# Layer 0's attention order worked out by a planner from a table; initial loads and boundary loads put in another order

## The chip, the cores and the metric

The kernel runs on one core of one Trainium2 chip. Its engines are TensorE (PE), VectorE (DVE), ScalarE (ACT), GpSimd (POOL) and SyncE (SP, which here only issues DMAs). The metric is the device time of one execution in microseconds.

## The reference, cut to what matters

Sixteen samples of 128 channels by 32x32 pixels (1024 tokens) pass through two blocks, each a mixing step and a second step, both with residuals:

```
x = x + linear_attention(group_norm(layer_norm_c(x)))      # layer 0
t = t + stu(layer_norm(t))          # t: x as 1024 tokens
x = x + conv3x3_block(layer_norm_c(x))                     # layer 1
t = t + routed_experts(layer_norm(t))
```

The attention of layer 0 makes queries, keys and values by a 128x128 projection, takes a softmax of the queries over tokens and of the keys within each of four heads, forms a 32x32 context for each head, applies it to the queries and projects the result. The STU is a causal convolution of the tokens with 16 spectral filters, through a Fourier transform, followed by learned 128x128 matrices, plus three taps of direct matrices:

```
U = irfft(rfft(phi) * rfft(u));  out = sum_k U_k s_k M_phi[k]     # plus and minus filters
out = out + sum_i shift(u, i) @ M_u[i]
```

The STU is computed for the first 1024, 512, 256 and 128 tokens with four sets of matrices and mixed with weights. Layer 1 applies two 3x3 convolutions with batch norm and ReLU, then an expert layer: a softmax over tokens for each of 64 experts, the eight largest tokens of each, and two matrices for each expert.

## The kernel before, in words

**Layer 0, attention stage** (0 to 395.7 us). One sample is an object of the class `Attention`, whose methods are its operations, each a handful of instructions on one engine. In order of dependence: `tokens` (eight transposes on PE of 128x128), `moments`, `tokens_copy`, `variance`, `root`, `scales`, `norm` (the layer norm, one ACT instruction for each block of 128 columns, L141), `spread`, `group`, `group_var`, `group_root`, `group_scale` (the group norm's scale), `channels` (transposes back), `channels_copy` (which yields `xn`, L409), `q_`, `q_max`, `q_exp`, `k`, `k_max`, `k_sub`, `k_exp`, `k_sum`, `k_recip`, `k_scale` (on POOL, L461), `q_tokens`, `q_copy`, `context` (PE, L482), `context_mask`, `fold`, `fold_copy`, `fold2`, `fold2_copy` (which fold the values' and the output's weights into one 128x128 matrix), `out`, `out_add`. Then the STU's forward part: `input` (transposes), `input_copy` (ACT, L530), `moments2` to `norm2`, `even` and `odd` (PE, the Fourier transform of the even and odd residue classes of time, L551), copies and sums on ACT and DVE, `even_turns` to `odd_turns4` (butterflies on POOL, which end with the store of the spectrum to `vd` in DRAM, L607), `taps_in` (transposes, L159 as a helper's line), `taps_copy`, `taps` (24 matmul records a sample, L618) and `taps_add` (DVE, L625, then the store of x to `xd`, L626).

The order of the work is written out by hand: `period` (L713) has 62 entries, each an operation and a depth, and the loop at L731 runs periods, doing in period p each operation for sample p + depth. PE, DVE, ACT and POOL execute in the program's order (`manual_schedule(engines=PINNED)`); SP isn't pinned there, and a scheduler of the framework places its DMAs. PSUM is three tiles of 128x1024 (`big`) and two small ones (`s`).

Two generators are stepped by the same loop. `filters()` (L628), once a period at the entry `filters`, negates half the filter's table (`wfm`), transforms the filters (even and odd matmuls at L636), and then loads and scales one of 16 parts of the spectral matrices in each step: the load of `mi` (L662) is issued in the step before the one that uses it (L665, L667). `prepare()` (L671), one step at the start of each period, loads the convolution weights (`raw`), scales and combines them on POOL (L683 to L693), stores them in DRAM as `cwd`, and scales the table of the inverse transform (`pwi`, L703, stored as `wid`).

At the start SP issues the loads of x0, x1, `wf`, `phi`; later x loads are issued by `tokens`, two samples ahead, into eight buffers.

**Layer 0, generation and multiplication** (395.7 to 684.3 us, L746 to L842): in 16 chunks c of frequencies, PE generates the filter's matrices and multiplies the samples' spectra by them; each chunk's products are stored to `yd` by two DMAs of 512 KB (L839). The last two chunks' products go into `yd[1]`.

**Boundary** (684.3 to 723.9 us): SP loads `wi` (the inverse transform's table, from `wid`), `cw` (convolution weights, from `cwd`) and small vectors. `load(b)` (L940) loads a sample's x from `xd` and its products y in two parts: part 0 from the first fourteen chunks (L945, 896 KB), part 1 from the last two (128 KB). For sample 0 the x and part 0 go through POOL's queue, the rest through SP's.

**Layer 1**: the class `Routed` has the operations of one sample, and `table` (L1263) lists each of them with engine, estimated duration, due time, what it depends on, which buffers it opens and closes. `planned` (L1475) plays a list schedule: of the operations that could start within 0.25 us of the earliest, it takes the one due first (due plus b times the period, 54.66), and returns all of them in the order of their planned starts. `ready` gives the earliest time for operations without dependencies. The loop at L1345 then issues them, SP pinned too. The first operations of a sample are `even` (POOL, L958), `odd`, `odd_turn`, `odd_out` (DVE, L965 to L985), `inverse` (PE, L1039), `add` (DVE, L1048) and `tokens`; the convolutions are L926. The experts (L1367 to L1472) follow.

Of the kernel before, what the change touches and what calls it, by code (L numbers as in the profile page):

```python
# [1 line left out]

# [6 lines left out]
F32 = mybir.dt.float32  # L9
# [57 lines left out]
def metaformer_kernel(ctx: ExitStack, tc: tile.TileContext, io: dict, out: bass.AP):  # L67
# [96 lines left out]
    with ExitStack() as l0:  # L164
# [41 lines left out]


        with ExitStack() as a0:
# [96 lines left out]
            for b in range(2):  # L305
                load(b)
            wqk = aconst.tile([P, 2 * C], F32, name="wqk")
# [16 lines left out]
            nc.vector.tensor_scalar(mu[:, 0], mu[:, 0], wmix[:, 0:1], None, ALU.mult)  # L324
            for i in range(1, NF):
                nc.vector.scalar_tensor_tensor(
                    mu[:, i], mu[:, i], wmix[:, i : i + 1], mu[:, i - 1], ALU.mult, ALU.add
                )

# [11 lines left out]
            class Attention:  # L341
# [10 lines left out]
                def tokens(self):  # L352
                    if self.b + 2 < B:
                        load(self.b + 2)
                    self.x = xt[self.b]
                    self.pt = big().rearrange("p (j c) -> p j c", c=C)
                    transpose_in(self.pt, self.x)
# [34 lines left out]
                def norm(self):  # L392
                    normalize(self.tok, self.tok, self.sts[:, 0], self.sts[:, 3])
# [19 lines left out]
                def q_(self):  # L413
# [17 lines left out]
                def k(self):  # L431
# [69 lines left out]
                def fold2(self):  # L501

                    self.pw = ps.tile([P, P], F32, name="pw", tag="s")
                    nc.tensor.matmul(self.pw, wv, self.wy, start=True, stop=True)

                def fold2_copy(self):
# [39 lines left out]
                def norm2(self):  # L546
                    normalize(self.ub, self.ub, self.sts2[:, 0], self.sts2[:, 3])
# [64 lines left out]
                def taps(self):  # L612

                    self.pa = big()
                    for si, (lo, hi) in enumerate(SEGS):
                        for tap in range(KU):
                            a = max(lo, tap)
                            nc.tensor.matmul(  # L618
                                self.pa[:, a:hi], mu[:, NF - 1 - si, tap, :],
                                self.u[:, a - tap : hi - tap],  # L620
                                start=(tap == 0), stop=(tap == KU - 1),
                            )
# [5 lines left out]
            def filters():  # L628

                wfm = setup.tile([P, NQ // 2, 2 * P], F32, name="wfm", tag="mi")  # L630
                nc.vector.tensor_scalar(wfm, wf[:, 1::2, :], -1.0, None, ALU.mult)

                def values(q, dst):
                    for sgn in range(2):
                        w = wfm[:, q // 2, :] if sgn and q % 2 else wf[:, q, :]
# [4 lines left out]
                yield  # L640
                xf = spectrum_tile()
                for parity in range(2):
                    pe = class_values(parity, values)
                    t = class_copy(pe, 1)
                    ts = class_copy(pe, ROT) if parity else t
                    ab = class_sums(parity, pe, t)
                    class_differences(parity, ab, pe, ts)
                    yield
                    for part in range(2):
                        butterflies(ab, xf, parity, part)  # L650
                    if parity:
                        butterflies(ab, xf, 1, butterflies(ab, xf, 1, 2))
                    yield
                half = CW // 2
                e, o = (xf[:, :, i].rearrange("p c r m j -> p c (r m j)") for i in range(2))
                nc.vector.tensor_tensor(ph[:, :, :half], e, o, ALU.add)
                nc.vector.tensor_tensor(ph[:, :, half:], e, o, ALU.subtract)
                for m in range(EPR // MB):
                    es = slice(m * MB, (m + 1) * MB)
                    for i in range(NF):  # L660
                        mi = setup.tile([P, MB, C], F32, name="mi", tag="mi")
                        nc.sync.dma_start(mi, io["M_phi"][i, :, es, :])  # L662
                        yield
                        if i == 0:
                            nc.vector.tensor_scalar(mst[:, es, :], mi, coef[:, 0:1], None, ALU.mult)  # L665
                        else:
                            nc.vector.scalar_tensor_tensor(  # L667
                                mst[:, es, :], mi, coef[:, i : i + 1], mst[:, es, :], ALU.mult, ALU.add
                            )

            def prepare():  # L671
# [36 lines left out]
            nc.sync.dma_start(wf, io["wf"])  # L708
            phi = spool.tile([P, NQ, 2, P], F32, name="phi", tag="xf")
            nc.sync.dma_start(phi, io["phi"])  # L710


            period = (  # L713
                ("q_max", 3), ("out_add", 1), ("tokens", 6), ("moments", 6), ("context", 2),
                ("channels", 4), ("input", 1), ("norm2", 0), ("context_mask", 2),
                ("group_root", 4), ("k_exp", 3), ("fold", 2), ("group_scale", 4), ("moments2", 1),
# [884 lines left out]
```

## Time and profile before

Three runs took 1327.79, 1319.41 and 1328.11 us; the median is 1327.79.

| | us |
|---|---|
| profiled execution, its own time | 1324.0 |
| its span | 1322.2 |
| PE busy | 1216.7 (92%) |
| DVE busy | 907.2 (69%) |
| ACT busy | 705.2 (53%) |
| POOL busy | 503.3 (38%) |
| attention stage, 0 to 396: PE busy | 359.6 of 396 |
| generation and multiplication, 396 to 684: PE busy | 278.5 of 288 |
| boundary, 684 to 724: PE busy | 19.5 of 40 |
| layer 1's convolutions and routing, 724 to 1212: PE busy | 475.1 of 488 |
| experts and output, 1212 to 1322: PE busy | 84.1 of 110 |

Rows of the timeline read: start, duration, engine, line of the kernel, instruction, output <- input, size, count; in brackets how long the engine was idle before and what released it. Matmuls overlap, so differences of starts, not the durations, give PE's work. Where the line of a helper stands (L132 statistics, L141 normalization, L149, L154 and L159 transposes, L232 and L241 sums), the tile's name tells the operation. A chain row has start, length and what it was.

### The profile page before, as it was taken

The page shows a single profiled execution, that of the slowest core. Times are in us where ns is not written, and L with a number is a line of the kernel's source. Part 1 is how long each engine was busy: PE and PEld are TensorE (multiplying, and loading weights), DVE is VectorE, ACT ScalarE, POOL GpSimd, SP SyncE. Part 2 cuts the span into 40 slices and gives each one's busy share as a digit, 9 for nine tenths or more (in the row PEclk, how much of TensorE's full clock was granted, in tenths as well). Part 3 has the DMA queues.
Part 4 walks back from the last instruction along what each step waited for, and adds up shares of the span by engine and source line. Part 5 has one row for each costly group of instructions (what it writes and reads, how often), then busy time and mean ns, then how long its engine had stood idle before and what let it go on. Part 6 is the DMA issues. An engine that isn't in the chain of part 4 may idle for free. (4 is left out here: it accounts for less than half of the span.)

```text
span 1322.2 us, 33734 instructions
## 1 busy us (share of the span) xinstructions
PE 1216.7 (92%) x14116; PEld 990.8 (75%) x14116; DVE 907.2 (69%) x1982; ACT 705.2 (53%) x1424; POOL 503.3 (38%) x816
## 2 busy tenths in 40 slices
PE   4889999999998999999956999999999999996886
PEld 3777777777767888888846987989888888883443
DVE  5688887877765666776637767777778676772224
ACT  3777777777545666666623435545555454544111
POOL 2324545454685777777743111222212121110002
PEclk8899999999998999999987999999999999997998
DMA  7014343433344333333367211313122113007986
GB/s 268 17 35 140 118 134 112 144 124 121 114 149 145 127 125 127 127 121 119 107 235 182 70 48 49 88 27 111 32 80 64 33 49 127 17 24 260 374 329 255
DMA packets 87401, 162.99 MB, mean 123 GB/s; under 512 B 5584, under 2 KB 40784, under 8 KB 86864
## 3 DMA queue, kind: packets, MB, share of 16 engines
q1 hardware_dynamic: 86608, 158.33, 36.2%
q8 instruction: 111, 1.82, 0.6%
q0 software_dynamic: 640, 2.49, 0.5%
q14 instruction: 42, 0.34, 0.1%
HBM read 104.18 MB, written 56.62 MB: 122 GB/s over the span
## 5 line engine op out<-in xcount | busy, mean ns | idle before, releaser
L926 PE MATMUL pcv<-v,cw 128*128 128x256 f32 x1536 | 342.9, 380 | 0.0
L926 PEld LDWEIGHTS pcv<-v,cw 128*128 128x128 f32 x1536 | 286.8, 190 | 42.2 <-issue 5.7
L785 ACT COPY g<-pg 128x512 f32<-128x512 f32 x288 | 153.1, 591 | 102.8 <-PE pg L776 102.8
L783 DVE COPY g<-pg 128x512 f32<-128x512 f32 x224 | 145.8, 687 | 90.1 <-PE pg L776 90.1
L776 PE MATMUL pg<-ph,mst 32*128 32x128 f32 x4096 | 155.3, 287 | 4.5 <-ACT g L785 3.0
L776 PEld LDWEIGHTS pg<-ph,mst 32*128 32x128 f32 x4096 | 130.7, 190 | 30.8 <-issue 25.9
L796 PE MATMUL py<-g,v 128*32 128x128 f32 x4096 | 140.1, 276 | 3.8 <-POOL v L768 1.2
L796 PEld LDWEIGHTS py<-g,v 128*32 128x32 f32 x4096 | 105.3, 110 | 20.7 <-issue 2.4
L767 POOL TENSOR_TENSOR v<-xc 128x256 f32<-128x256 f32 x128 | 91.6, 741 | 71.6 <-PE py L796 62.5
L141 ACT ACTIVATE tok<-tok,sts 128x128 f32<-128x128 f32 x256 | 101.8, 481 | 23.8 <-POOL sts L1001 20.4
L132 DVE BATCH_NORM_STATS2 bst<-big 128x6 f32<-128x256 f32 x256 | 91.1, 417 | 19.5 <-PE big L154 12.1
L1066 POOL TENSOR_SCALAR sts<-bst 128x8 f32<-128x8 f32 x16 | 6.5, 406 | 235.7 <-DVE bst L132 235.7
L920 DVE TENSOR_TENSOR v<-pads 128x544 f32<-128x544 f32 x128 | 85.0, 723 | 9.9 <-ACT pads L1119 9.5
L618 PE MATMUL big<-u,mu 128*128 128x128 f32 (+4 forms) x384 | 86.0, 380 | 0.0
L274 POOL TENSOR_TENSOR xf<-ab 128x256 f32<-128x256 f32 x34 | 24.8, 730 | 132.0 <-DVE ab L241 131.9
L618 PEld LDWEIGHTS big<-u,mu 128*128 128x128 f32 x384 | 56.7, 191 | 18.0 <-issue 15.4
L1097 ACT ACTIVATE ct<-pcv,bn 128x256 f32<-128x256 f32 x64 | 30.3, 474 | 68.8 <-PE pcv L926 67.9
L551 PE MATMUL big<-wf,ub 128*128 128x256 f32 x256 | 62.0, 385 | 0.2
L149 PEld LDWEIGHTS big<-ident,x 128*128 128x128 f32 x384 | 47.3, 148 | 19.2 <-issue 7.2
L149 PE MATMUL big<-ident,x 128*128 128x128 f32 x384 | 53.6, 286 | 8.5 <-DVE x L1048 3.4
L1115 DVE TENSOR_TENSOR r<-pcv,cs 128x256 f32<-128x256 f32 x64 | 26.9, 420 | 49.0 <-PE pcv L926 48.2
L141 ACT ACTIVATE tt<-tt,sts 128x128 f32<-128x128 f32 x128 | 51.1, 480 | 9.2 <-POOL sts L1001 8.9
(231 smaller groups left out, 2271.3 us busy)
## 6 DMA issues: line engine op xcount, KB each, us to landing
we<-in_weight SPq DMA_DIRECT2D x32, 1024.0 KB, 9.7
vd<-xf SPq DMA_DIRECT2D x16, 1024.0 KB, 5.1
xc<-vd SPq DMA_DIRECT2D x64, 256.0 KB, 3.5
yd<-ys SPq DMA_DIRECT2D x32, 512.0 KB, 3.8
y<-yd SPq DMA_DIRECT2D x15, 896.0 KB, 6.5
x<-in_x SPq DMA_DIRECT2D x16, 512.0 KB, 4.1
mi<-in_M_phi SPq DMA_DIRECT2D x16, 512.0 KB, 4.9
xd<-x SPq DMA_DIRECT2D x16, 512.0 KB, 6.0
```

The lines of the kernel that those rows point to most:

```text
L132: nc.vector.bn_stats(bst[:, j : j + 2, :].rearrange("p j s -> p (j s)"), src[:, j : j + 2, :].rearrange("p j c -> p c j"),)
L141: nc.scalar.activation(dst[:, j, :], src[:, j, :], AF.Identity, bias=nm[:, j : j + 1], scale=r[:, j : j + 1],)
L149: nc.tensor.transpose(pt[:, j, :], src[:, j * P : (j + 1) * P], ident)
L551: nc.tensor.matmul(dst, self.ub[:, q, :], wf[:, q, :], start=True, stop=True)
L618: nc.tensor.matmul(self.pa[:, a:hi], mu[:, NF - 1 - si, tap, :], self.u[:, a - tap : hi - tap], start=(tap == 0), stop=(tap == KU - 1),)
L767: nc.gpsimd.tensor_tensor(vv[:, x, 1:, bs], e, o, op)
L776: nc.tensor.matmul(pg[r][:, i], mst[rs, 4 * q + i, :], ph[rs, c, :], start=True, stop=True,)
L783: nc.vector.tensor_copy(dst, src)
L785: nc.scalar.copy(dst, src)
L796: nc.tensor.matmul(py[rows, x, kl, :], v[:, (x * NM + m) * JL + jl, 1 - ri : 3 - ri, :] .rearrange("p k b -> p (k b)"), g[:, ((x * 2 + ri) ...
L920: nc.vector.tensor_tensor(v[:, k], d[i], d[j], op)
L926: nc.tensor.matmul(pc[:, i], wt[:, dy, k, :], v[:, k, hf * HR + dy : hf * HR + dy + HR], start=(dy == 0), stop=(dy == 2),)
```

## The change

1. The attention's order comes from a second `table` and `planned`; `period`, the depths and `filters()` are gone. `norm`, `norm2` and `taps` are cut into two operations each; the filters' steps become operations `f_mixes` to `f_values` (once) and `f_matrix` (sixteen times, load and use in one operation), and `prepare` an operation that takes two steps of its generator. `ready` gives arrival times to the operations that need loads. `q_`, `k` and `fold2` are renamed `queries`, `keys` and `refold`. The filters' steps use the same PSUM and work buffers as the samples.
2. SP's loads at the start are issued as x0, x1, `wf`, `phi`, x2 to x7; from sample 8 on, `tokens` issues the load of the sample two ahead, as before.
3. At the boundary x0 and part 0 of y0 go through SP's queue, ahead of the store of the second-last chunk; `wi` follows, and `cw` comes after y1. SP's resulting order is: small vectors, x0, y0 part 0, store of chunk 14, `wi`, store of chunk 15, y0 part 1, x1, y1, `cw`, x2, y2. Before it was: `gw` and others, `wi`, `cw`, store of chunk 14, store of chunk 15, y0 part 1, x1, y1, x2, y2.
4. Layer 1's `table` has other due times, its period is 51.23, and `ready` is 7 + 5 min(b, 3) for every sample.
5. `planned` passes the operation's name to `ready` and frees a tile only if it was opened; `perform` replaces the list of two-part names; `Routed.x` and `.y` become properties.

The order that `planned` gives for the attention begins as follows on three engines (operation.sample; prepare.k is the k-th pair of steps):

```
PE:   tokens.0 tokens.1 group.0 channels.0 f_even.0 group.1 queries.0 keys.0 tokens.2 q_tokens.0 channels.1 f_odd.0 group.2 queries.1 keys.1 tokens.3 context.0 q_tokens.1 fold.0 channels.2 tokens.4 queries.2 refold.0 q_tokens.2 context.1 out.0 fold.1 group.3 keys.2 input.0
DVE:  ... k_sum.0 k_recip.0 variance.2 scales.2 spread.2 f_matrix.0 f_matrix.1 group_var.2 f_odd_sums.0 q_max.1 group_scale.2 k_max.1 q_recip.1 context_mask.0 k_sub.1 f_values.0 k_sum.1 q_max.2 k_recip.1 fold_copy.0
POOL: f_even_turns.0 prepare.0 prepare.1 k_scale.0 prepare.2 prepare.3 prepare.4 f_odd_turns.0 prepare.5 prepare.6 prepare.7 prepare.8 k_scale.1 prepare.9 prepare.10 prepare.11
```

and a later period on PE is: `out.7 group.10 channels.9 tokens.11 input.7 queries.9 context.8 keys.9 fold.8 q_tokens.9 taps0.6 taps_in.7 refold.8 taps1.6 even.7 odd.7`.

The diff, cut to its core:

```diff
             for b in range(2):
                 load(b)
+            nc.sync.dma_start(wf, io["wf"])
+            phi = spool.tile([P, NQ, 2, P], F32, name="phi", tag="xf")
+            nc.sync.dma_start(phi, io["phi"])
+            for b in range(2, 8):
+                load(b)
...
                 def tokens(self):
-                    if self.b + 2 < B:
+                    if 8 <= self.b + 2 < B:
                         load(self.b + 2)
...
-                def norm(self):
-                    normalize(self.tok, self.tok, self.sts[:, 0], self.sts[:, 3])
+                def norm(self, i):
+                    half = NT // 2
+                    normalize(
+                        self.tok, self.tok, self.sts[:, 0], self.sts[:, 3], i * half, (i + 1) * half
+                    )
 
...
+                def taps(self, i):
+
+                    if i == 0:
+                        self.pa = big()
+                    taps(self.pa, mu, self.u, i)
 
...
+                def f_odd_sums(self):
+                    fl.ao = class_sums(1, fl.po, fl.ot)
+                    class_differences(1, fl.ao, fl.po, fl.os)
+
+                def f_odd_turns(self):
+                    for part in range(2):
+                        butterflies(fl.ao, fl.xf, 1, part)
+                    butterflies(fl.ao, fl.xf, 1, butterflies(fl.ao, fl.xf, 1, 2))
+
+                def f_values(self):
+                    half = CW // 2
+                    e, o = (fl.xf[:, :, i].rearrange("p c r m j -> p c (r m j)") for i in range(2))
+                    nc.vector.tensor_tensor(ph[:, :, :half], e, o, ALU.add)
+                    nc.vector.tensor_tensor(ph[:, :, half:], e, o, ALU.subtract)
+
+                def f_matrix(self):
+                    m, i = divmod(self.b, NF)
                     es = slice(m * MB, (m + 1) * MB)
-                    for i in range(NF):
-                        mi = setup.tile([P, MB, C], F32, name="mi", tag="mi")
-                        nc.sync.dma_start(mi, io["M_phi"][i, :, es, :])
-                        yield
-                        if i == 0:
-                            nc.vector.tensor_scalar(mst[:, es, :], mi, coef[:, 0:1], None, ALU.mult)
-                        else:
-                            nc.vector.scalar_tensor_tensor(
-                                mst[:, es, :], mi, coef[:, i : i + 1], mst[:, es, :], ALU.mult, ALU.add
-                            )
+                    mi = setup.tile([P, MB, C], F32, name="mi", tag="mi")
+                    nc.sync.dma_start(mi, io["M_phi"][i, :, es, :])
+                    if i == 0:
+                        nc.vector.tensor_scalar(mst[:, es, :], mi, coef[:, 0:1], None, ALU.mult)
+                    else:
+                        nc.vector.scalar_tensor_tensor(
+                            mst[:, es, :], mi, coef[:, i : i + 1], mst[:, es, :], ALU.mult, ALU.add
+                        )
+
+                def prepare(self):
+                    for _ in range(2):
+                        next(preparing, None)
+
+            fl = SimpleNamespace()
 
...
-            period = (
-                ("q_max", 3), ("out_add", 1), ("tokens", 6), ("moments", 6), ("context", 2),
...
+            def ready(b, name):
+
+                if name == "tokens":
+                    return 2.0 * b if b < 2 else 8.5 + 1.5 * b
+                if name == "f_matrix":
+                    return 25.0 + 6.0 * b
+                if name == "prepare":
+                    return 22.0 + 3.0 * b
+                return inputs.get(name, 0.0)
+
+            inputs = dict(f_mixes=6.5, f_negate=6.0, f_even=9.5, f_odd=9.5)
+
+            table = (
+                ("tokens", "PE", 0.88, -286.5, "", "big:X x", ""),
...
+                ("k_scale", "POOL", 1.95, -245.9, "k_recip", "", ""),
+                ("context", "PE", 1.77, 119.9, "q_copy k_scale", "s:c", "ke qt"),
+                ("context_mask", "DVE", 0.32, -62.7, "context q_recip", "", "s:c"),
...
+                ("input_copy", "ACT", 1.02, -368.2, "input moments2", "ub", "big:u"),
...
+                ("taps_in", "PE", 0.88, -435.1, "norm21", "big:U", "ub"),
+                ("taps_copy", "ACT", 1.02, -453, "taps_in", "u", "big:U"),
...
+                ("taps 0", "PE", 2.65, 233.5, "taps_copy f_mixes", "big:r", "u"),
+                ("taps 1", "PE", 2.65, -270.1, "taps0", "", "u"),
+                ("taps_add", "DVE", 1.25, -336.2, "taps1", "", "big:r x"),
...
+                ("f_odd_turns", "POOL", 5, -143, "f_odd_sums f_even_turns", "sd:f", "ab1:f sd:f"),
+                ("f_values", "DVE", 4.5, -272.1, "f_odd_turns", "", "xf:f"),
+                ("f_matrix", "DVE", 1.4, 82.7, "", "", ""),
+                ("prepare", "POOL", 1.7, -52, "", "", ""),
             )
-            reach = max(d for _, d in period)
-            samples, setting, preparing = {}, filters(), prepare()
+            buffers = dict(mi=2, big=3, x=8, tok=3, xn=3, qe=2, ke=2, qt=2, ub=2, u=2, et=2, ets=1, ab0=2, ab1=2, sd=2, xf=2, s=2)
+
...
             with tc.manual_schedule(engines=PINNED):
-                for p in range(-reach, B):
-                    next(preparing, None)
-                    for name, d in period:
-                        b = p + d
-                        if name == "filters":
-                            next(setting, None)
-                        elif 0 <= b < B:
-                            if name == "tokens":
-                                samples[b] = Attention(b)
-                            getattr(samples[b], "q_" if name == "q" else name)()
+                for b, name in planned(
+                    table, buffers, B, 102.38, left_out, ready
+                ):
+                    if b not in samples:
+                        samples[b] = Attention(b)
+                    perform(samples[b], name)
...
         wi = first.tile([P, NQ, 2, P], F32, name="wi", tag="wi")
-        nc.sync.dma_start(wi, wid)
         cws = first.tile([P, 2, 3, 4, C], F32, name="cw", tag="cw")
         cw = [cws[:, n] for n in range(2)]
-        for n in range(2):
-            nc.sync.dma_start(cw[n], cwd[n])
...
+        def load_x(b):
+            if b not in loaded:
+                loaded.add(b)
+                xt[b] = xpool[b > 0].tile([P, N], F32, name=f"x{b}", tag=f"x{b}")
+                nc.sync.dma_start(xt[b], xd[b])
+
+        def load_y(b, i):
+            js = (slice(P - 2 * JL), slice(P - 2 * JL, P))[i]
+            if i == 0:
+                yts[b] = first.tile([P, 2, 2 * NM, C], F32, name="y", tag="y", bufs=2)
+            nc.sync.dma_start(
+                yts[b][js].rearrange("p r x e -> p r (x e)"),
+                yd[i][:, :, b].rearrange("j r x e -> j r (x e)"),
+            )
+
         def load(b):
-            xt[b] = xpool[b > 0].tile([P, N], F32, name=f"x{b}", tag=f"x{b}")
-            (nc.sync if b else nc.gpsimd).dma_start(xt[b], xd[b])
-            yts[b] = first.tile([P, 2, 2 * NM, C], F32, name="y", tag="y", bufs=2)
-            for i, js in enumerate((slice(P - 2 * JL), slice(P - 2 * JL, P))):
-                (nc.gpsimd if b + i == 0 else nc.sync).dma_start(
-                    yts[b][js].rearrange("p r x e -> p r (x e)"),
-                    yd[i][:, :, b].rearrange("j r x e -> j r (x e)"),
-                )
-
+            load_x(b)
+            for i in range(2):
+                load_y(b, i)
+
+
+        loaded = set()
+        load_x(0)
+        load_y(0, 0)
+        nc.sync.dma_start(wi, wid)
 
 
...
+        def ready(b, name):
+            return 7.0 + 5.0 * min(b, 3)
+
+        order = planned(table, buffers, B, 51.23, left_out, ready)
         with tc.manual_schedule(engines=PINNED | {mybir.EngineType.SP}):
-            for b in range(2):
-                load(b)
+            load_y(0, 1)
+            load(1)
+            for n in range(2):
+                nc.sync.dma_start(cw[n], cwd[n])
             samples = [None] * B
             for b, name in order:
...
-            if closers[o] == 0:
+            if closers[o] == 0 and o in held:
                 slot, i = held.pop(o)
```

## The prediction

> **What bounds the kernel now.** I first read busy time by stage (columns: stretch and length, then busy us and instructions of PE, PEld, DVE, ACT, POOL, then clock, DMA share, GB/s).
>
> ```profile
> 0.00:66.00 66.00, 44.28 (x207) 35.87 (x208) 38.72 (x138) 36.58 (x78) 19.39 (x32) 0.87 0.38 143
> 66.00:102.00 36.00, 31.68 (x203) 25.36 (x202) 30.49 (x82) 26.67 (x55) 11.55 (x16) 1.00 0.10 32
> 102.00:318.00 216.00, 209.21 (x1247) 164.14 (x1246) 175.35 (x423) 155.87 (x323) 103.96 (x166) 1.00 0.41 128
> 318.00:396.00 78.00, 74.42 (x407) 56.74 (x409) 54.48 (x98) 42.59 (x86) 51.18 (x87) 1.00 0.43 135
> ```
>
> In the attention stage PE is the bound from 102 us on; DVE, next, has 19% spare. Only the fill (0 to 102) is loose. The timeline of DVE gives the period: the first, second, tenth and eleventh samples' `taps_add`.
>
> ```profile
> 100.26 1.23 DVE L625 TENSOR_TENSOR x<-big,x 128x1024 f32<-128x1024 f32 x1 [1.28 <-PE big L618]
> 122.14 1.23 DVE L625 TENSOR_TENSOR x<-big,x 128x1024 f32<-128x1024 f32 x1 [1.28 <-PE big L618]
> ...
> 297.24 1.23 DVE L625 TENSOR_TENSOR x<-big,x 128x1024 f32<-128x1024 f32 x1 [1.27 <-PE big L618]
> 318.25 1.22 DVE L625 TENSOR_TENSOR x<-big,x 128x1024 f32<-128x1024 f32 x1 [1.35 <-PE big L618]
> ```
>
> So (297.24 - 100.26) / 9 = 21.89 us per sample. From start to start in PE's timeline one sample's work is 20.77 us (taps 5.21, the four projections and the context 1.7 to 1.8 each, even and odd 1.75, five transposes 0.88, the rest 0.6). About 1.1 us of each period is idle. The largest piece shows in the waits of PE from 102 to 318:
>
> ```profile
> PE big L159 <- ACT ub L530: 6.6, 10, 0.7
> ```
>
> `taps_in` waits 0.7 us in each of ten periods, for the freeing of a PSUM buffer that `input_copy` reads. Then the fill, 0 to 70 us (waits: total, times, longest):
>
> ```profile
> POOL ke L461 <- DVE qs L469: 26.3, 2, 23.2
> POOL raw L683 <- DMA raw<-in_w: 14.0, 1, 14.0
> ...
> PE big L636 <- DMA phi<-in_phi: 5.6, 1, 5.6
> ```
>
> POOL stands 23 us before the first `k_scale`; the second comes at 62.44:
>
> ```profile
> 51.80 1.92 POOL L461 TENSOR_TENSOR ke<-ke,ks 128x1024 f32<-128x1024 f32 x1 [23.20 <-DVE qs L469]
> ...
> 62.44 1.92 POOL L461 TENSOR_TENSOR ke<-ke,ks 128x1024 f32<-128x1024 f32 x1 [3.08 <-DVE qs L469]
> ```
>
> Generation and multiplication (396 to 684, PE 97%) and layer 1 after 724 (475.06 of 488 us) are PE's. Between them PE starves: the chain that ends in the first convolution, then PE's timeline:
>
> ```profile
> 684.71 6.60 DMA yd<-ys
> 691.42 0.64 SPq L945
> ...
> 693.38 9.03 DMA y<-yd
> ```
>
> ```profile
> 694.76 1.19 PE L1039 MATMUL big<-wi,y 128*128 128x128 f32 x4 [13.46 <-DMA y<-yd]
> ```
>
> The last product's store takes 6.60 us to land, and all else follows.
>
> [...] the load goes out 0.11 us after the 6.60. [...] While its two boundary loads (8.4 and 10.9 us to landing) were under way, all queues together moved at most 420 GB/s.
>
> **The change part by part.** I followed the new order with before's durations; no stage computes more.
>
> *Steady attention.* In the new PE order `taps_in` stands after both halves of `taps`, so the PSUM wait lies behind 5.2 us of work. I find no new late operand: a matrix load has about a period's slack against a landing of 4.9 us, x loads over 10 us. DVE has 17.8 us of work per period. I take 20.85 us (20.77 and 0.08 of hand-overs), bounds 20.77 and 21.5. Against 21.89 over nine periods that is -9.4, and -0.3 in the two of 21.01 that follow: **-9.7 us**. The halved norms and taps cost nothing: the helper already issues one instruction per 128 columns.
>
> *Fill.* The first normalized sample is ready at about 22.8 instead of 33.56, for the filters no longer stand ahead of it on ACT and DVE. Then three new waits come:
> 1. `f_matrix.1` stands on DVE ahead of the odd filters' sums, and its load must wait until `f_odd` (ending at 35.5) has freed the buffer; landing 4 to 5 us, multiply 1.4. `tokens.3` needs the PSUM that those sums free: PE idle to 42.85, **3.25**.
> 2. `f_values` on DVE stands ahead of `fold_copy.0` and waits for the odd turns on POOL, which stand behind the second `raw` load (lands 45.8, turns 46.8 to 51.8): `refold.0` at 57.35, **5.5**.
> 3. `k_scale.1` stands on POOL behind prepare 5 to 8, two generator steps each: five operations of 1.0, one of 2.1, and the first two scalings of `pwi` (0.6 and 0.9, L703). The load of `pwi` waits on SP behind the stores of the second `cwd` (issued at 60.2, lands at 65). So `k_scale.1` ends at 68.4, and `context.1` starts at 68.45 after **9.5** idle[...].
>
> Done by 68.45: five tokens 4.4, groups 0.45, three channels 2.64, filters 7.44, three queries 5.16, two keys 3.58, three q_tokens 2.64, context and folds 2.22, together 28.5. Before, at its own `context.1` at 67.34, the same count gives 32.2 and so 33.3 at 68.45: 4.8 behind. From 66 to 102 the kernel before is idle 36 - 31.68 = 4.3; I count 2.3 after [...]. The fill thus costs **+2.8**; each of three landings by its shortest or longest in the trace gives 0 to +8. For second steady periods with a short hand-over late I add **+1.6** (0 to 3). Attention: -9.7 + 2.8 + 1.6 = **-5.3**. Its tail is as dense as before; I take nothing.
>
> *Loads at the start.* All eight x loads were issued in the first 13.4 us before too, and the filter tables once: nothing gained; `raw` behind x is in wait 2.
>
> *Boundary.* x0 and the first part of y0 move from POOL's queue (issued at 674.57 and 676.44) to SP, at about 671, ahead of the second-last products' store (678.61); `wi` (1 MB) goes between the two stores, `cw` (1.5 MB) behind y1. The last store no longer shares the engines with y0, and 512 KB stores land in 3.8 us at the median: gain 6.60 - 3.8 = 2.8 at best. `wi`, issued at 679.4 with 5.4 us to land, is nearly out of the way. First inverse, y1 and what follows move together. `cw`, issued near 692, has until 720 and took 9.1 us; on SP it stands before x2 and y2, worth 3.9 us at 400 GB/s against some 4 us of cover. I take **-2.7**, bounds -4 and +2.
>
> *Layer 1.* New due times and arrivals leave PE's order nearly as it was, and the first operations and the last sixty of every engine are the same. Pairs of samples stand 60.68 us apart for 60.1 us of PE work; nothing is left to win: **0**, bounds -2 and +3. `perform`, the two properties and the planner's guard move no time.
>
> Sum -5.3 - 2.7 = -8.0. The profiled execution's own time is 1324.0 us (span 1322.2), which gives 1316. The median is 1327.79, of runs from 1319.41 to 1328.11; I go half that way: **1318 us**.
>
> **Rivals.**
> - *The fill is cheap.* If prepare's loads land in the 2.3 us that is the shortest here and the waits 2 and 3 shrink, the fill costs nothing, and the period is 20.77: -10.8, boundary -4, layer 1 -2, so -17: **1309**. For: the head start of 11 us on the first sample. Against: three loads in line before `k_scale.1`.
> - *The fill eats the gain.* Fill +8, hand-overs +3, boundary 0: -9.7 + 11 = +1, **1327**. For: POOL and SP now carry prepare in one convoy, and each late landing is PE's. Against: two of the stores overlap POOL work.
> - *Slower: DVE stops at the matrix loads.* Load and use of a matrix stood one period apart in the code before; now `f_matrix` issues both, SP sends the load among stores that wait for POOL and DVE, and DVE is the fullest engine after PE. If each of the 14 remaining matrices holds DVE beyond its spare, this turns to a loss from 8 / 14 = 0.6 us each; at 1.6 us each it is +22 - 8 = +14: **1340**. Against: each load needs only the buffer of the matrix two before, a period earlier.
> - *It does not do what it says*: the x loads were early already; this is inside the forecast.
>
> **How the numbers follow.** Forecast 0.5, cheap fill 0.25, eaten gain 0.13, slower 0.12. A difference under 1%, 13 us, can hardly be told from none: faster by that means under 1314.5, which takes the cheap fill and a sixth of the forecast; slower, over 1341, about half of the last rival and surprises in layer 1. Chances 0.33, 0.56, 0.11. Cutting a tenth at either end gives 1302 to 1333.
>
> **What would show it.** `taps_add` 20.8 to 20.9 apart; no PE wait on `input_copy`; the first xn near 23 us; `context.1` on PE near 68 after some 9 us idle; the last attention matmul near 389 instead of 394.2; the last store landing in about 4 us, the first convolution near 716 (by 5.3 and 2.7 earlier than 723.91); layer 1's pairs still 60.7 apart. Wrong would be: periods above 21.3, DVE waiting for `mi` past 100 us, PE waiting for `cw` or y2, or a gain in layer 1.

## The result, and the profile after

The changed kernel took 1329.32 us at the median (1324.12 to 1333.71, 20 runs) against 1323.45 for the kernel before (20 runs): a ratio of 1.0046, 95% interval 1.0029 to 1.0064. Timed once more it was 1.0010 (0.9985 to 1.0035). The forecast's sum was 8 us faster; by these two ratios it is 6.1 and 1.3 us slower, and the second can't be told from no change. The profiled execution took 1326.42 us, its span 1324.3.

By stage, from the two profiles (the lengths of a stretch are differences of starts in the timelines and the chain):

| | before | after | difference | forecast |
|---|---|---|---|---|
| start of generation | 395.76 | 397.37 | +1.6 | -5.3 |
| from there to the issue of the last product store | 288.58 | 287.75 | -0.8 | 0 |
| from there to the first convolution | 39.41 | 45.23 | +5.8 | -2.7 |
| rest of the span | 598.45 | 593.95 | -4.5 | 0 |

The code of the second stage and of the experts is the same in both kernels; from the convolution near 1100 us to the end, the runs below take from 217 to 225 us. The rows that can be read are the first and the third.

Busy time by stage, columns as before:

```profile
0.00:66.00 66.00, 38.06 (x194) 29.49 (x194) 45.48 (x136) 35.04 (x72) 30.71 (x40) 0.90 0.54 193
66.00:102.00 36.00, 28.83 (x174) 23.99 (x175) 25.12 (x66) 24.45 (x53) 15.62 (x17) 0.89 0.16 61
102.00:318.00 216.00, 212.82 (x1266) 167.97 (x1265) 187.65 (x441) 162.46 (x337) 101.50 (x167) 1.00 0.40 127
318.00:396.00 78.00, 77.42 (x421) 58.83 (x419) 49.50 (x97) 41.94 (x80) 41.85 (x74) 1.00 0.28 92
```

From 102 to 396 PE is now idle 3.8 us instead of 10.4: the steady part did what the change is made for. PE's waits there no longer have the ten of `taps_in` for `input_copy`. Up to 102 PE is busy 66.9 us instead of 76.0, and from 66 to 102 its clock is lower (0.89 instead of 1.00). Two waits of PE from 0 to 110 us stand out. In the kernel before the longest wait of the first kind was 2.9 us, and there was none of the second:

```profile
PE pw L518 <- DVE wy L513: 8.8, 1, 8.8
...
PE pc L496 <- POOL ke L475: 8.2, 1, 8.2
```

They are the predicted waits before `refold.0` (L518) and before `context.1` (L496). POOL's timeline shows what is behind them (start, length, instruction):

```profile
47.17 1.00 POOL L723 TENSOR_TENSOR raw<-raw,srow 128x384 f32<-128x384 f32 x1 [6.62 <-DMA raw<-in_w]
48.13 0.72 POOL L286 TENSOR_TENSOR xf<-ab 128x256 f32<-128x256 f32 x1
...
55.77 1.85 POOL L725 TENSOR_TENSOR pcw<-raw 128x384 f32<-128x384 f32 x1
...
67.03 1.50 POOL L743 TENSOR_SCALAR pwi<-pwi,seg 128x128 f32<-128x128 f32 x2 [5.04 <-issue]
68.51 1.91 POOL L475 TENSOR_TENSOR ke<-ke,ks 128x1024 f32<-128x1024 f32 x1
```

POOL waits 6.6 us for the second `raw` load with the odd filters' turns (L286 to L308) behind it, then stands 5.0 us with `k_scale.1` behind. The row names no releaser for these 5.0 us, but the load of `pwi` was issued at 62.63 and took up to 4.3 us to land, which is 66.9. The planner couldn't see either wait: `prepare.4` and `prepare.8` each issue a load and use it in the same operation, to which the table gives 1.7 us, and `ready` lets them start at 34 and 46.

At the boundary the chain has both long transfers still:

```profile
685.48 6.67 DMA yd<-ys
...
694.08 9.51 DMA y<-yd
```

and after them something new shows in DVE's timeline and then in PE's:

```profile
715.37 0.43 DVE L1088 TENSOR_TENSOR zt<-y 128x256 f32<-128x256 f32 x1 [4.53 <-DMA y<-yd]
...
718.57 1.22 DVE L1177 TENSOR_TENSOR x<-big,x 128x1024 f32<-128x1024 f32 x1
```

```profile
719.89 1.94 PE L150 MATMUL big<-ident,x 128*128 128x128 f32 x8 [8.10 <-issue]
```

`odd.2` (L1088) waits for y2 on DVE; `add.1` (L1177) stands behind it, `tokens.1` (L150) waits for `add.1`, and `image.0`, whose normalization ended at 716.40, stands behind `tokens.1` on PE. In the kernel before the same transposes started earlier:

```profile
713.95 1.06 PE L149 MATMUL big<-ident,x 128*128 128x128 f32 x8 [2.41 <-ACT tok L141]
```

### The profile page after: what moved, and what is told of

Same layout as the page of the kernel before. It is cut to its first block, busy times and chain, and to the rows that moved or that the text cites. A ratio compares the mean times of both kernels' runs of the same rounds, so it can differ in the third digit from the quotient of the medians.

```text
span 1324.3 us, 33751 instructions
## 1 busy us (share of the span) xinstructions
PE 1211.2 (91%) x14116; PEld 989.4 (75%) x14116; DVE 916.8 (69%) x1982; ACT 706.9 (53%) x1424; POOL 504.9 (38%) x814
## 5 line engine op out<-in xcount | busy, mean ns | idle before, releaser
L1028 DVE TENSOR_TENSOR v<-pads 128x544 f32<-128x544 f32 x128 | 85.7, 729 | 15.8 <-ACT pads L1248 13.5
L475 POOL TENSOR_TENSOR ke<-ke,ks 128x1024 f32<-128x1024 f32 x16 | 34.5, 2156 | 132.2 <-DVE ks L472 61.4
L150 PE MATMUL big<-ident,x 128*128 128x128 f32 x384 | 52.9, 283 | 12.3 <-issue 8.1
L150 PEld LDWEIGHTS big<-ident,x 128*128 128x128 f32 x384 | 45.6, 146 | 17.8 <-issue 11.8
```

The lines of the kernel that those rows point to most:

```text
L150: nc.tensor.transpose(pt[:, j, :], src[:, j * P : (j + 1) * P], ident)
L1028: nc.vector.tensor_tensor(v[:, k], d[i], d[j], op)
```

## The experiments

Theory 1 is on the boundary: `cw`'s 1.5 MB, ahead of x2 and y2 on SP's queue, make y2 late. Theory 2 is on the fill: the steps of `prepare`, which the planner packs together early, put two loads in line ahead of `k_scale.1`. Their rivals stand in the expectations. Both are read by three figures: the start of generation (the attention with its fill), from the issue of the last product store to the first convolution (the boundary, "stretch"), and the run's time.

### The boundary: `cw` behind y2, and the old order

cw_after_y2, the changed kernel with:

```diff
-            for n in range(2):
-                nc.sync.dma_start(cw[n], cwd[n])
...
                     load(self.b + 2)
+                if self.b == 0:
+                    for n in range(2):
+                        nc.sync.dma_start(cw[n], cwd[n])
```

> The changed kernel with the two cw loads issued after x2 and y2 (in the first inverse) instead of ahead of them. Theory 1 (cw's 1.5 MB stand on SP's queue ahead of y2; y2 lands at 715.3, odd.2 on DVE waits for it ahead of add.1, and PE waits 8.1 us for tokens.1 ahead of image.0): DVE's wait of 4.5 us for y2 and PE's 8.1 us go, the stretch from the issue of the last product store to the first convolution falls from 45.4 us to 39 to 41, the time falls by 4 to 6 us. Rival (the boundary is late for another reason, the landing of the last store or wi): stretch and time stay within 1 us. Rival (cw is then late itself): the first convolution waits for cw and the stretch stays above 44 us.

bound_old, the changed kernel with:

```diff
         wi = first.tile([P, NQ, 2, P], F32, name="wi", tag="wi")
+        nc.sync.dma_start(wi, wid)
...
+        for n in range(2):
+            nc.sync.dma_start(cw[n], cwd[n])
...
-                nc.sync.dma_start(xt[b], xd[b])
+                (nc.sync if b else nc.gpsimd).dma_start(xt[b], xd[b])
```

(and the same for part 0 of y0; the two later loads of `wi` and `cw` are taken out).

> The changed kernel with the boundary loads put back as in the kernel before (wi and cw first, x0 and part 0 of y0 on POOL's queue, before the store of chunk 14); attention and layer 1 stay changed. Theory 1: the stretch from the issue of the last product store to the first convolution is 39 to 40.5 us as in the kernel before (39.6), the time falls by 5 us against the changed kernel, and about 1 us of a loss against the kernel before is left. Rival (layer 1's new due times cause the 8.1 us of idle PE): the stretch stays at 44 or more.

By its ratio to the kernel before the first came to 1.0026 (1.0007 to 1.0045), the second to 0.9999 (0.9979 to 1.0018). The changed kernel's first timing is 1.0046, so cw_after_y2 won 2.6 us by these figures, less than the forecast 4 to 6 and with overlapping intervals; against its second timing, 1.0010 (below), it won nothing. The wait for y2 went in both. PE's timeline of cw_after_y2 has, where 8.10 us stood:

```profile
713.46 1.07 PE L150 MATMUL big<-ident,x 128*128 128x128 f32 x8 [2.42 <-ACT tok L142]
```

and its stretch is 40.0 us, that of bound_old 39.1. New in cw_after_y2 is a wait of 4.80 us of DVE for y3, which is now behind `cw`. The new due times of layer 1 are in both kernels, so they are not what made the 8.1 us.

How large the loss is was less clear, since the later kernels, with the changed boundary untouched, gave other stretches. So the changed kernel was profiled again:

> The changed kernel itself once more, for a second profile of its boundary. If the late y2 belongs to the order of the loads, DVE waits over 1 us for y2 ahead of add.1, PE stands over 4.5 us before tokens.1, and the stretch from the last product store to the first convolution is above 41 us again; if it was an accident of one run, the stretch is 39 to 40 us.

Its stretch was 37.0, with 0.92 us of DVE's wait and 3.45 of PE's: neither of the two cases as I had put them, since the waits are there and the stretch is short. Over all runs the two orders are told apart by the wait, not by the stretch of one run:

| order of loads | DVE waits for y2 | PE idle before `tokens.1` | stretch |
|---|---|---|---|
| changed, eight profiles | 0.9 to 4.5 | 3.4 to 8.1, mean 5.9 | 37.0 to 45.2, mean 41.1 |
| before, five profiles | 0 to 0.3 | 2.4 to 2.8, mean 2.5 | 38.8 to 39.4, mean 39.1 |

Then both were timed on one chip:

> The changed kernel itself, timed beside bound_old_timed on one chip. If the new boundary order costs 6 us as the times of bound_old suggested, its time is 4 to 8 us above bound_old_timed's; if the 45.2 us of the first profile were rare (the four profiles with this order show 45.2, 41.9, 38.5 and 37.0 us from the last product store to the first convolution, against 39.1 to 39.4 with the old order in four), it is 0 to 2.5 us above.

> The changed kernel with the old boundary loads, for the same comparison: stretch 39 to 40 us again; time 1.000 of the kernel before by the first timing.

1327.66 us and ratio 1.0010 (0.9985 to 1.0035) against 1323.12 and 0.9989 (0.9971 to 1.0007): 0.2% or about 2.8 us by the ratios, near the 41.1 - 39.1 = 2.0 of the profiles. The two intervals overlap, so the times alone don't show a loss; the wait for y2, present in all eight profiles of the one order and at most 0.3 us in the five of the other, is what shows it. My estimate of the cost is 2 us on average. The stretch varies by 8 us between the eight profiles, and the first was the worst of them.

### The boundary: why the last store did not land sooner

wi_late, the changed kernel with:

```diff
         load_y(0, 0)
-        nc.sync.dma_start(wi, wid)
...
             load_y(0, 1)
+            nc.sync.dma_start(wi, wid)
             load(1)
```

> The changed kernel with wi loaded after the last product store and part 1 of y0 instead of between the two stores, so that the last store has no other transfer beside it. If the store's 6.67 us are wi's share of the DMA engines (my prediction's step, mis-sized by wi), it lands in 3.5 to 4.5 us; if the store takes that long by itself, it still needs over 5.5 us. The first inverse then waits for wi, so the time is no reading: the stretch grows by some 2 to 6 us.

The chain of this kernel shows the last store with nothing beside it:

```profile
685.68 3.56 DMA yd<-ys
```

So the store needs 3.56 us alone (3.55 in spread_wi_late below, which has the same edit); in the fourteen other profiles, with other transfers under way, it took 5.4 to 7.7. I had expected a longer stretch. It was 37.1 us (the last store issued at 685.31, the first convolution at 722.43): with `wi` issued at 689.95 the first inverse started at 695.30, no later than the 695.85 of the changed kernel. One of the eight profiles above has 37.0 without this edit, so this single run shows how the store lands, and not a gain of the stretch.

### The fill: `prepare` out of the way

prep_spread, the changed kernel with:

```diff
+                    if name == "prepare":
+                        continue
                     perform(samples[b], name)
+                    if name == "odd_turns4":
+                        samples[b].prepare()
```

> The changed kernel with every prepare operation taken from its planned place and issued after odd_turns4 of its sample, so that none stands on POOL before the first sample's butterflies; all else keeps its planned order. Theory 2 (the fill is lost to prepare's steps and loads on POOL, behind which f_odd_turns.0 and k_scale.1 stand): PE's wait before refold.0 (8.8 us) falls to under 5 and that before context.1 (8.2 us) to under 2; the start of generation moves from 397.4 to 386 to 391 and the time falls by 6 to 11 us. Rival (f_matrix.1 on DVE is what makes the odd filters late, and PE meets the next wait there): the waits fall by less than 5 us together and the time by under 4. Rival (the steps of prepare in the later periods now hold k_scale and the butterflies of the steady state): the first taps_add comes some 10 us earlier but periods grow by over 0.5 us.

Generation started at 383.80, 13.6 us earlier than in the changed kernel; the ratio to the kernel before is 0.9908 (0.9870 to 0.9946). Against the changed kernel's second ratio, 1.0010, that is 13.5 us. PE's timeline around the two places:

```profile
52.39 0.49 PE L518 MATMUL pw<-wy,wv 128*128 128x128 f32 x2 [1.72 <-DVE wy L513]
53.23 1.10 PE L150 MATMUL big<-ident,qe 128*128 128x128 f32 x8 [0.34 <-ACT qe L441]
54.31 2.05 PE L496 MATMUL pc<-ke,qt 128*128 128x128 f32 x16
```

`context.1` starts at 54.31 instead of 70.47. The third forecast also holds in part: with a pair of steps in every period, nine periods of `taps_add` took 21.84 us each (85.76 to 282.34) against 21.39 in the changed kernel, so 4 us of the 17.6 won at the first `taps_add` were given back.

prep_fm_spread, the same and:

```diff
+                    if name == "f_matrix":
+                        if b >= 2:
+                            Attention.f_matrix(SimpleNamespace(b=b - 2))
+                        continue
...
+                    if name == "taps_add" and b in (8, 9):
+                        Attention.f_matrix(SimpleNamespace(b=b + 6))
```

> As prep_spread, and each f_matrix operation is issued at the planned place of the second next one (the last two after taps_add of samples 8 and 9), so that no matrix load stands in the fill before the odd filters' sums. Theory 2 with both parts: against prep_spread the wait of 2.7 us on PE before group.2 and the rest before refold.0 go, the start of generation comes 2 to 4 us before prep_spread's. Rival (f_matrix.1 costs nothing beside the rest): within 1 us of prep_spread.

Generation started at 385.93, 2.1 us later than in prep_spread, and the ratio is 0.9913 (0.9881 to 0.9945), the same: its rival's forecast. With `prepare` out of the way, moving `f_matrix` won nothing more.

### The fill: each wait by itself

turns_first issues prepare.4 after `f_odd_turns.0`, kscale_first issues prepare.5 to 8 after `k_scale.1`, both_first issues 4 to 8 after `k_scale.1`. The edit of turns_first; in the others the list of operations and the pair of sample and name are as told:

```diff
+                    if name == "prepare" and b in (4,):
+                        continue
                     perform(samples[b], name)
+                    if (b, name) == (0, "f_odd_turns"):
+                        for i in (4,):
+                            samples[b].prepare()
```

> The changed kernel with one operation moved: prepare.4 (the second raw weights' first scaling, which waits for their load) is issued on POOL after f_odd_turns.0 instead of ahead of it. Theory 2 in its strong form (the two long waits of PE stand in one chain on POOL and SP: the second raw load, then its stores, then the load of pwi, then k_scale.1): PE's wait before refold.0 falls from 8.8 to under 3 us, but the one before context.1 grows by about as much, since k_scale.1 still ends near 70; context.1 starts at 68 to 71 and generation at 396 to 399, no gain over 2 us. Rival (each wait is worth its own length): context.1 starts near 64 and generation 5 to 7 us earlier.

> The changed kernel with k_scale.1 issued on POOL ahead of prepare.5 to prepare.8 instead of behind them; prepare.4 stays ahead of the odd filters' turns. Theory 2, strong form: PE's wait before refold.0 stays near 8 us, the one before context.1 goes (under 1.5 us), context.1 starts at 61 to 63, generation starts 7 to 9 us earlier than 397.4, and the time falls by 6 to 9 us. Rival (prepare's steps, now behind k_scale.1, hold up k_scale.2 or the butterflies instead): the gain is under 4 us.

> The changed kernel with both moves on POOL at once: f_odd_turns.0 and k_scale.1 ahead of prepare.4 to prepare.8, which follow k_scale.1. turns_first gave 3.4 us of the start of generation and kscale_first 8.3. If the two waits are one chain, k_scale.1 moves to 54 to 56 and generation starts at 384 to 387 (their sum, 11.7, below 397.4), as with all of prepare spread out; if the steps of prepare behind k_scale.1 then hold k_scale.2, PE waits over 3 us before context.2 and generation starts at 388 or later. Time 0.991 to 0.995 of the kernel before.

| | wait before `refold.0` | wait before `context.1` | `context.1` | generation | ratio to before |
|---|---|---|---|---|---|
| changed kernel | 8.8 | 8.2 | 70.47 | 397.37 | 1.0046 (1.0029 to 1.0064); again 1.0010 (0.9985 to 1.0035) |
| turns_first | 1.7 | 9.1 | 65.95 | 393.95 | 0.9997 (0.9973 to 1.0021) |
| kscale_first | 6.1 | none | 60.92 | 389.04 | 0.9965 (0.9944 to 0.9985) |
| both_first | 1.7 | none | 55.50 | 386.91 | 0.9959 (0.9939 to 0.9980) |

turns_first lies between its two forecasts. The first wait is 7.1 us shorter, but PE came to it 2.4 us later, and the second wait grew by 1.0; `context.1` started 4.5 us earlier. By its time this kernel can't be told from the changed one's second timing. PE's timeline (the window ends inside the last row):

```profile
54.88 0.49 PE L518 MATMUL pw<-wy,wv 128*128 128x128 f32 x2 [1.72 <-DVE wy L513]
55.71 1.09 PE L150 MATMUL big<-ident,qe 128*128 128x128 f32 x8 [0.35 <-ACT qe L441]
65.95 1.44 PE L496 MATMUL pc<-ke,qt 128*128 128x128 f32 x5 [9.14 <-POOL ke L475]
```

What was won is the 4.7 us of odd turns that had stood in POOL's chain behind the load and now lie in front of it. kscale_first did what its theory said for the second wait and for generation; its first wait shrank too, from 8.8 to 6.1. both_first's sum would have been 397.4 - 3.4 - 8.3 = 385.7; it came to 386.9, with a wait of 2.81 us before `context.2`, for now `k_scale.2` stands behind the scaling of `pwi`, before which POOL stands for 5.28 us. Theory 2 holds: the fill's loss is the chain raw load, its stores, `pwi` load on POOL and SP, and `k_scale.1` at its end is the larger part.

### The attention alone, and versions that beat both

attn_only is bound_old with layer 1's old table, period 54.66 and old `ready`:

> The kernel before with the new attention order alone: boundary loads and layer 1's due times as before. Theory (the attention as changed is 1 to 3 us slower, and layer 1's new due times win 1.9 us between the first convolution and the convolution near 860 us): from the first convolution to that one 136.0 us as before against 134.2 with the new dues; the time is 1 to 3 us above bound_old's, ratio to the kernel before 1.001 to 1.003. Rival (the new dues win nothing outside that stretch and lose it later): same time as bound_old.

Its ratio is 1.0005 (0.9982 to 1.0029), against 0.9999 for bound_old: the new due times can't be told from the old ones by the time. In the chain, from the first convolution (722.52 in attn_only) to the one that starts at 858.41 there, it is 135.9 us, as before, against 134.0 to 134.3 in the kernels with the new ones. The attention and the order of the first loads are the only changes left in attn_only. It starts generation at 397.99, and the kernel is no faster and no slower than the one before within 0.3%.

spread_bound joins prep_spread and bound_old:

> prep_spread's attention with the boundary loads of the kernel before (bound_old), layer 1's new due times kept. If the two findings add: generation starts near 384 us as in prep_spread, the stretch from the issue of the last product store to the first convolution is 39 to 40 us, and the time is 2 to 5 us under prep_spread's, near 0.988 of the kernel before. Rival (cw ahead of y2 cost something only in the run profiled): same time as prep_spread.

0.9901 (0.9867 to 0.9935), not to be told from prep_spread; its stretch is 39.1.

spread_wi_late joins prep_spread, wi_late and cw_after_y2:

> prep_spread with two boundary edits on top: wi loaded after the last product store (which then landed in 3.56 us in wi_late) and cw after y2. Theory: stretch 36 to 38 us instead of 39 to 42, generation starts at 384 to 386, time 1308 to 1312, 0.987 to 0.990 of the kernel before. Rival (wi, late, holds up the first inverse by what the store gains): stretch 39 or more and the time of prep_spread, 0.991.

1306.68 us, 0.9867 (0.9830 to 0.9903), the lowest here, though six runs don't tell it from prep_spread (0.9870 to 0.9946). Generation starts at 385.49, 10.3 us earlier than in the kernel before; the stretch is 37.0, 2.4 less, near the 2.7 that I had forecast. The first inverse, at 680.30 there, now waits for `wi` and no longer for y0, with PE idle for 13.08 us before it.

## Why the prediction was wrong, by its steps

*Steady attention, forecast -9.7 + 1.6 = -8.1.* The right mechanism, too large: from 102 to the start of generation PE is idle 295.3 - 290.2 = 5.1 us after and 10.4 before, a gain of **5.3**. The wait for `input_copy` went. But I had taken a period of 20.85; nine took (295.91 - 103.39) / 9 = 21.39, and even the last two, which show hardly a wait, 21.1. The term for hand-overs (0.08) was mis-sized: the starts are 0.3 apart beyond the work. In the first seven periods PE also has small waits, 3.2 us in all.

*Fill, forecast +2.8.* This is the step that failed in size and turned the sign of the attention. The two waits came where I had put them, 59.49 for 57.35 and 70.47 for 68.45. What the sum missed is first that both ended 2.1 us later: the odd turns ended at 52.8 instead of 51.8, and `f_values` behind them took 1.6 us more than alone (last section). At 70.47 the kernel had done the 28.5 us that I counted for 68.45, and the kernel before 35.3: 6.8 behind instead of 4.8. Second, from 70.5 to 102 I let the changed kernel lose 2.3 us, which was my estimate, and the one before 4.3. The changed kernel was idle for 2.7, and `context.1` took 3.51 us (3.35 from its start to the next one) instead of 1.95 (1.78) in the kernel before at 67.34. The granted clock was 0.50 from 66 to 72, 0.61 from 72 to 74 and 1.00 from 74 to 102, where the kernel before had 1.00 from 66 to 102. With these 1.6 us it lost 4.3, as much as the kernel before. The fill cost **6.9** (the 1.6 of the later generation and the 5.3 gained after 102), not 2.8. The first profile is the mildest: seven others with the same attention start generation at 398.0 to 399.0, which would make it 7.5 to 8.5 against the one profile of the kernel before. The experiments show the same from the other side: with `prepare` out of the way generation comes 13.6 us earlier. The rival "the fill eats the gain" is the case that came, at the upper end of the bound that I had kept for this term. Of the three waits, the first came as 2.7 us before `group.2` and 0.5 before `tokens.3`, by chance together what I had summed (3.25). The 2.7 has another cause than `f_matrix.1`, whose move won nothing in prep_fm_spread: ahead of `group.2` three short DVE instructions of sample 2's statistics took 3.2 us longer beside instructions of POOL (last section); in prep_spread that wait is 1.2.

*Boundary, forecast -2.7.* Wrong in sign, and with 4.7 us the largest miss, by two of its sentences. "The last store no longer shares the engines": it lands in 3.56 us when alone and took 5.4 to 7.7 beside other transfers, so the mechanism was right, but `wi` "is nearly out of the way" was not. Issued at 680.03, it took 9.6 us here, beside both stores, instead of the 5.4 of the kernel before, and the last store took 6.67. And `cw`'s 3.9 us "against some 4 us of cover": the 3.9 was my estimate, 1.5 MB at 400 GB/s; the kernel before moved 386 to 420 GB/s in those 2 us windows between 674 and 690 where the DMA share was 0.95 or more (POOL's queue had its two boundary loads under way for most of that time). I had counted the cover of PE, but the wait fell on DVE, whose order puts `odd.2` ahead of `add.1`; what is late for an operation of sample 2 stopped sample 1 (4.53 us on DVE), and through PE's order sample 0 (8.10 us). The mean of the profiles is **+2.0**.

*Layer 1, forecast 0, bounds -2 and +3.* The new due times, which I said leave PE's order "nearly as it was", are worth 1.9 us at its start in the trace, inside the bound, and nothing that the times can tell.

*Sum.* +1.6 + 2.0 - 1.9 = +1.7 by these readings, between the two measured ratios (1.3 and 6.1 us). Of the part of the first figure beyond it I have no cause; the experts' stage drifts by more (217 to 225 us). The granted clock moves with the time (in the second timing 1318.3 us at 0.972 and 1332.09 at 0.961), and over the 20 runs of the first figure it averaged 0.963, where the kernel before had 0.967 to 0.969 in the four later timings; which of the two is the cause isn't shown. The slow rival, DVE stopped by the matrix loads past 100 us, didn't come: DVE has no wait for `mi` there.

## What to carry to other kernels

A planner that is given compute times but no landing times of loads fills an idle engine with operations that wait for DMAs, and what is planned behind them in that engine's order waits too: here the odd turns behind POOL's 6.6 us for `raw`, and `k_scale.1` behind the 5.0 us before the scaling of `pwi`. Look for the first operation of the bound engine's chain that stands behind a load. Two waits in one chain aren't worth their lengths: 8.8 and 8.2 us of waiting gave 10.5 when both were gone. Shorten the chain's end first (8.3 us here), not the wait that shows first (3.4). When transfers are reordered, ask for each which operation reads it, and what stands behind that operation on its own engine, not only when the bound engine needs it: y2 behind `cw` held DVE for 4.5 us and PE for 8.1 in the first profile.

## What the runs showed of the hardware that I had not expected

The two DVE instructions of `f_values`, an addition and a subtraction of 128x1024 with both operands in SBUF, took 1.21 and 1.22 us in the kernel before and in prep_spread. POOL stood idle meanwhile in both. From prep_spread:

```profile
46.09 1.21 DVE L690 TENSOR_TENSOR ph<-xf 128x1024 f32<-128x1024 f32 x1
```

In the changed kernel POOL's `prepare` ran at the same time:

```profile
52.84 2.00 DVE L690 TENSOR_TENSOR ph<-xf 128x1024 f32<-128x1024 f32 x1 [6.61 <-POOL xf L308]
54.77 2.01 DVE L691 TENSOR_TENSOR ph<-xf 128x1024 f32<-128x1024 f32 x1
```

and POOL's addition at 55.77 took 1.85 us, where the same line took 0.99 at 34.83. So both sides slowed beside each other, by two thirds and by nearly double. This added 1.6 us to the first wait, which ended 2.1 later than forecast. turns_first, whose POOL was busy from 47.11 to 52.94, has 1.57 and 2.02 us for the same two instructions at 48.58 and 50.06; both_first, whose POOL was idle from 45.8 to 53.5, has 1.22 for each.

Shorter instructions of the changed kernel show the same. On POOL, then on DVE:

```profile
32.97 1.91 POOL L475 TENSOR_TENSOR ke<-ke,ks 128x1024 f32<-128x1024 f32 x1 [3.62 <-ACT sts L120]
34.83 0.99 POOL L725 TENSOR_TENSOR pcw<-raw 128x384 f32<-128x384 f32 x1
```

```profile
33.10 1.80 DVE L126 SCALAR_TENSOR_TENSOR sts<-sts 128x8 f32<-128x8 f32 x1
34.93 0.91 DVE L127 SCALAR_TENSOR_TENSOR sts<-sts 128x8 f32<-128x8 f32 x1
```

These two DVE instructions have eight columns and take 0.17 us each at 61.58 and 61.78. Here the first ends at 34.90, POOL's at 34.88; the second ends at 35.84, POOL's at 35.82. A third, L392, started at 35.97 beside POOL's L727, which ran from 35.90 to 36.90, took 0.96 and ended at 36.93, where it takes 0.16 at 62.07. So in these rows each of the three, started while POOL's instruction ran, ended 0.02 or 0.03 us after it, however short it is by itself. The DVE instructions of `f_values` and POOL's beside them end in turn: DVE's first at 54.84, the second of two scalings on POOL at 55.69 (it took 1.98 us, where others take 1.00), DVE's second at 56.78, POOL's addition at 57.62. Why they do is not shown.
